# A network with a bidirectional Mamba as its last layer: a block's preparation in other steps of a hand-written schedule, outputs gated in place, GpSimd's products in other states

## The chip, the cores and the metric

One core of a Trainium2 chip runs the whole network in one launch. The time is device microseconds of the program; smaller is better. Engines are named as in the profile: PE (TensorE, matmul), DVE (VectorE), ACT (ScalarE), POOL (GpSimd), SP (SyncE, which here only issues DMAs). Each engine works through its own queue in order and waits on semaphores for the others.

## The reference

The input is (2, 128, 56, 56) in float32. Four layers, each added to its input: an agent attention, a 3x3 convolution, a mixture of experts on 2x2 patches, and a Mamba that runs in both directions along each row of the image. The change is in the last layer alone. Cut to what it computes, for one direction (`f` along the row, `b` against it), with L = 56, 256 inner channels and 16 states:

```python
xz = x @ in_w.T                       # x: (112 rows, 56, 128)
xi, z = jnp.split(xz, 2, axis=-1)
xc = silu(conv_b + sum(xp[:, k:k + L, :] * conv_w[:, k] for k in range(4)))
dt, Bm, Cm = jnp.split(xc @ xproj_w.T, [8, 24], axis=-1)
dt = softplus(dt @ dt_w.T + dt_b)
def step(h, inp):
    dt_l, B_l, C_l, u_l = inp
    h = exp(dt_l[:, :, None] * A) * h + (dt_l * u_l)[:, :, None] * B_l[:, None, :]
    return h, jnp.einsum('bds,bs->bd', h, C_l)
y = (ys + xc * Dp) * silu(z)
out = y @ out_w.T
```

Both directions' outputs are joined, multiplied by `fuse_w`, normalized over the channels and added to x.

## The kernel before, in words

**Blocks, ways, pairs, units.** The 112 rows of the two images are cut into 14 blocks of 8 rows (BLK = 448 positions). A block has two *ways*, f and b (class `Half`). A way has 16 *units*: unit u is the pair of states j = u // 2 and the half of the channels m = u % 2. The 128 partitions hold 64 channels times the two states of the pair, and the two groups of 64 channels (r) lie one after another, so that each unit works on 128x896 values. There are 14 x 2 x 16 = 448 units.

**What a unit does.** `decay` (L1820, ACT, twice 128x448): dA = exp(A dt), into one of two PSUM buffers. `push` (L1831, POOL): dBu = dtu times B, into one of four buffers. `scan` (L1853, DVE): the recurrence, into the tile h of the pair. After the second unit of a pair comes the *C product*, h times the row of C (128x1792): on DVE (L1862) it reads C from PSUM bank `c`, where `read_out` (L1841, PE) spreads it; on POOL (L1859), for the pairs listed in `POOLED`, it reads C from SBUF, where `send_low` has spread it by DMA (L1750). `collect` (L1873, PE) adds the two states and accumulates over the pairs into y in PSUM; the first one adds the skip term (L1869). After a way's last unit `close` (L1879, DVE) multiplies y by the Silu of the gate.

**What a way needs first.** `norm` (L1610, ACT; once for a block); `conv(0)`, `conv(1)` (L1703 PE, L1712 ACT); `silu` (L1884 to L1887, ACT: a table load, the Silu of this way's xc and, at the same time, of the block before's gates zs, and a table load back); `low` (PE, ACT L1735); `send_low` (SP: low to DRAM, then B and C spread to all partitions); `step(m)` (L1755 PE, four activations L1765 to L1769 on ACT); `error(m)` (L1775, DVE); `log(m)` (L1780, ACT); `softplus(m)` (L1785 PE, L1786 ACT); `weigh` (L1793, POOL: dtu = dt xc, into the tile `sp_u`; then a small memset of dt, L1797); `send_steps` (L1808, SP: four DMAs for dtu, four for dt, which bring them into the units' layout); `gate(m)` (L1720 PE, L1727 ACT).

**What follows a block.** `fuse` (L1624 PE, L1635 ACT), `measure` (L1641, L1643, DVE statistics), `root` (L1648, L1649, ACT), `newton` (L1657 to L1661, DVE), `normalize` (L1665, ACT), `turn_back` (L1676 PE, L1680 ACT), `onto` (L1686, POOL: the sum with x; L1688, the DMA out).

**What sets the order.** Within the scheduled part each engine's queue is the order in which the program text calls it. The main loop goes over the 448 units. For unit n it issues: `decay` of unit n+1; the *fetches* due at n (the copy out of PSUM that a stage before has left over); `push` of unit n+3; `scan` of unit n with its C product; `close` of a way that is through; `read_out` at even units of pairs not on POOL; `collect` of the unit three before (a quota lets it fall one behind at unit 3 and catch up later); then `run(n)`, the stages booked for step n. `book(at + k, ...)` puts a stage at step k counted from the start of the block before (32 steps a block: 0 to 15 its f units, 16 to 31 its b units, 32 and on the block's own units). `tag` says which of two PSUM banks the stage uses, `mm` or `c`, which it shares with the read-outs; its fetch comes one step later, or two with `late=1`. The tables of these steps, written by hand for the first block and in the `else` branch for all others, are what the change rewrites.

Buffers that matter: `sp_u` one for both ways, `zs` (the gates) one for f and two for b, `yv` (the gated output) one for each way, `Cs` one for each way with all its pairs, `Bs` two, `h` four, `dBu` four, `dA` two.

Of the kernel before, what the change touches and what calls it, by code (L numbers as in the profile page):

```python
# [8 lines left out]
F32 = mybir.dt.float32  # L9
# [1427 lines left out]

MAMBA_STATES, MAMBA_RANK, MAMBA_TAPS = 16, 8, 4

POOLED = {"f": (0, 3, 6), "b": (0, 3)}  # L1440


class MambaWeights:
# [88 lines left out]
def mamba_pair(net, out, wts, combine):  # L1532
# [19 lines left out]
    with ExitStack() as ctx:  # L1552
# [137 lines left out]
        class Half:  # L1690


            def __init__(self, blk, w):
                self.blk, self.w = blk, w
                self.dA, self.dBu, self.hc = {}, {}, {}

            def conv(self, m):
                w = self.w
# [17 lines left out]
            def gate(self, m):  # L1716
                pm = mm("gate_ps")
                if m == 0:
                    self.zs = work.tile([P, 2, BLK], F32, name="zs", tag=f"zs{self.w.d}", bufs=1 if self.w.d == "f" else 2)
                nc.tensor.matmul(  # L1720
                    rows(pm[:, :BLK]),
                    self.w.gate[:, m, :],
                    self.blk.xn[:, :, K - 1 : K - 1 + HW],
                    start=True,
                    stop=True,
                )
                return lambda: nc.scalar.copy(self.zs[:, m, :], pm[:, :BLK])  # L1727
# [8 lines left out]

            def send_low(self):

                pooled = self.w.pooled
                far = dram.tile([2 * S, BLK], F32, name="far", tag="far")  # L1740
                nc.sync.dma_start(far, self.lo[R:, :])
                self.B = work.tile([P, PAIRS, BLK], F32, name="Bs", tag="Bs")
                self.C = work.tile([P, len(pooled), BLK], F32, name="Cs", tag=f"Cs{self.w.d}", bufs=1)
# [90 lines left out]

            def read_out(self, u):

                r = R + S + u // 2 * 2
                self.c_ps = ps.tile([P, 512], F32, name="c_ps", tag="c")
                for s in range(2):
                    one_row = net.ident[:LOW, r + s : r + s + 1].to_broadcast([LOW, H])  # L1840
                    nc.tensor.matmul(self.c_ps[s * H : (s + 1) * H, :BLK], one_row, self.lo, start=True, stop=True)  # L1841

            def scan(self, u):

                j, m = self.unit(u)
                if m == 0:
                    self.hc[j] = work.tile([P, 2, 2, BLK], F32, name="h", tag="h", bufs=4)
                h = self.hc[j]
                hf, bf = (v.rearrange("p r t -> p (r t)") for v in (h[:, m], self.dBu[u]))
                af = self.dA[u][:, : 2 * BLK]  # L1850
                if self.w.d == "b":
                    hf, af, bf = hf[:, ::-1], af[:, ::-1], bf[:, ::-1]
                nc.vector.tensor_tensor_scan(hf, af, bf, 0.0, ALU.mult, ALU.add)  # L1853
                if m == 1:
                    shape = [P, 4, BLK]
                    h4 = h.rearrange("p m r t -> p (m r) t")
                    if self.by_pool(u):
                        c = self.C[:, self.w.pooled.index(j), :].unsqueeze(1).to_broadcast(shape)
                        nc.gpsimd.tensor_tensor(h4, h4, c, ALU.mult)  # L1859
                    else:  # L1860
                        c = self.c_ps[:, :BLK].unsqueeze(1).to_broadcast(shape)
                        nc.vector.tensor_tensor(h4, h4, c, ALU.mult)  # L1862

            def collect(self, u):
                j, m = self.unit(u)
# [9 lines left out]
                    )  # L1875

            def close(self):
                self.yv = work.tile([P, 2, BLK], F32, name="yv", tag=f"yv{self.w.d}", bufs=1)
                nc.vector.tensor_mul(self.yv, self.y[:, :, :BLK], self.zs)  # L1879

        def silu(inputs, gates):

            if inputs:
                nc.scalar.activation(inputs.xc, inputs.xc, AF.Silu)  # L1884
            if gates:
                nc.scalar.activation(gates.zs, gates.zs, AF.Silu)
            nc.scalar.preload_act_table_set(EXP_LN)  # L1887
# [5 lines left out]
        def book(step, *stages, tag="mm", late=0):  # L1893

            agenda.setdefault(step, []).extend((stage, tag, late) for stage in stages)

        for n, blk in enumerate(blocks):
# [31 lines left out]
                book(11, b.weigh, b.send_steps)  # L1929
            else:  # L1930
                before = blocks[n - 1]
                book(at + 6, blk.norm)
                book(at + 7, lambda f=f: f.conv(0))
                book(at + 8, lambda f=f: f.conv(1), late=1)
                book(at + 10, lambda f=f, g=before.ways[0]: silu(f, g))
                book(at + 12, lambda b=b: b.conv(0))
                book(at + 12, lambda b=b: b.conv(1), tag="c", late=1)
                book(at + 15, f.low, tag="c")
                book(at + 17, f.send_low)
                book(at + 17, lambda f=f: f.step(0))  # L1940
                book(at + 18, lambda b=b, g=before.ways[1]: silu(b, g))
                book(at + 19, lambda f=f: f.error(0))
                book(at + 19, lambda f=f: f.log(0))
                book(at + 20, lambda f=f: f.step(1))
                book(at + 21, lambda f=f: f.error(1))
                book(at + 22, lambda f=f: f.log(1))
                book(at + 22, lambda f=f: f.softplus(0), tag="c")
                book(at + 23, b.low)
                book(at + 24, lambda f=f: f.softplus(1))
                book(at + 25, f.weigh)  # L1950
                book(at + 26, lambda f=f: f.gate(0))
                book(at + 27, lambda b=b: b.step(0))
                book(at + 27, f.send_steps)
                book(at + 28, lambda b=b: b.error(0))
                book(at + 28, lambda b=b: b.log(0))
                book(at + 29, lambda b=b: b.step(1))
                book(at + 31, lambda b=b: b.error(1))
                book(at + 31, lambda b=b: b.log(1))
                book(at + 32, lambda b=b: b.softplus(0), tag="c")
                book(at + 33, lambda f=f: f.gate(1), late=1)  # L1960
                book(at + 33, lambda b=b: b.softplus(1), tag="c")
                book(at + 33, b.send_low)
                book(at + 35, lambda b=b: b.gate(0))
                book(at + 38, b.weigh)
                book(at + 43, b.send_steps)
                book(at + 46, lambda b=b: b.gate(1), late=1)

            at = STEPS * (n + 1)
            book(at + 4, lambda blk=blk: blk.fuse(0))
            book(at + 4, lambda blk=blk: blk.fuse(1), late=1)  # L1970
            book(at + 6, blk.measure)
            book(at + 7, blk.root, tag="c", late=1)
            book(at + 7, blk.newton)
            book(at + 15, blk.normalize)
            book(at + 16, blk.turn_back)
            book(at + 31, blk.onto)
        for h, step in zip(blocks[-1].ways, (10, 18)):
# [17 lines left out]
        with tc.manual_schedule(engines={E.PE, E.Activation, E.DVE, E.Pool, E.SP}):  # L1995
# [13 lines left out]
            for _ in second:  # L2009
                pass  # L2010
        with tc.manual_schedule(engines={E.PE, E.Activation, E.DVE, E.Pool, E.SP}):
            units[0][0].decay(0)
# [130 lines left out]
```

## Time and profile before

| | |
|---|---|
| median of 4 runs | 3104.88 us (3100.77 to 3114.65) |
| the profiled execution: time, span | 3106.7 us, 3104.9 us |
| granted TensorE clock over the span | 0.936 |
| the Mamba: first push; first scan; end of the last scan; last operation's end | 1736.8; 1738.9; 3077.0; 3092.8 us |
| start of scan 0 of the second block; of the last block | 1846.0; 2988.9 us |

The Mamba's 14 blocks take about 95 us each, the first 107. The page's busy times over the whole span mix the four layers; of the Mamba alone the groups of instructions, over the stretch from 2080 to 3000 us, say:

| line, engine, what | count | mean ns of one |
|---|---|---|
| L1831 POOL push, 128x896 | 310 | 2143 |
| L1853 DVE scan, 128x896 | 310 | 2006 |
| L1862 DVE C product, 128x1792 | 107 | 2021 |
| L1859 POOL C product, 128x1792 | 49 | 3992 |
| L1793 POOL weigh, 128x896 | 19 | 2108 |
| L1820 ACT dA, 128x448, two to a unit | 618 | 636 |
| L1884, L1887 ACT table loads | 38 | 1283 |
| L1879 DVE gating, 128x896 | 20 | 1084 |

Of the DMAs, dtu (224 KB) has a median of 3.9 us from issue to landing, dt 5.2, one C row pair's half (112 KB) 7.4, B (896 KB) 9.0. A mean is the time from an instruction's start to its end. Instructions that follow each other on an engine overlap a little, so their distance from start to start is a few hundredths of a microsecond less. A wait is put down to what released it last.

### The profile page before, as it was taken

To read this page: it belongs to the slowest core of one execution; us is meant where nothing else is said; L and a number is where in the kernel's file an instruction comes from. 1 tells how busy PE (TensorE), PEld (TensorE's weight loads), DVE (VectorE), ACT (ScalarE), POOL (GpSimd) and SP (SyncE) were. 2 spreads that over 40 slices of the span, in tenths; PEclk is the share of its full clock that TensorE was granted. 3 is DMA by queue.
4 is the path that set the end of the run, shared out by engine and by line. 5 is a ranking of instruction groups with operands and counts; after the bars stand their busy time and mean duration, and the time that the engine had idled before them with its cause. 6 is when DMAs were issued, how large, how long until landed. Compare 5 with 4: busy or idle time off the path is not lost. (4 is left out here: it accounts for less than half of the span.)

```text
span 3104.9 us, 34608 instructions
## 1 busy us (share of the span) xinstructions
PE 2822.4 (91%) x12964; PEld 1076.7 (35%) x12964; DVE 2225.3 (72%) x2033; ACT 1758.0 (57%) x2634; POOL 1500.3 (48%) x801
## 2 busy tenths in 40 slices
PE   7999999999898899999996789999889898889885
PEld 3333333332244444444443322333323333233321
DVE  5879999999886111111112699999999999999996
ACT  5778878877641011011111577776777777777764
POOL 3000100000511000000002799999999999999995
PEclk9999999999998899999997888989999999889987
DMA  1000000000011778777783553444444535434440
GB/s 54 1 1 1 1 1 1 1 1 1 1 36 44 309 284 318 293 308 308 290 316 104 114 103 81 91 103 93 96 89 87 105 82 114 91 81 91 95 101 8
DMA packets 133271, 333.65 MB, mean 107 GB/s; under 512 B 20228, under 2 KB 90340, under 8 KB 129492
## 3 DMA queue, kind: packets, MB, share of 16 engines
q1 hardware_dynamic: 111104, 303.96, 34.0%
q0 software_dynamic: 5520, 15.62, 1.6%
q10 hardware_dynamic: 16452, 11.61, 1.2%
q8 instruction: 106, 1.74, 0.2%
q14 instruction: 89, 0.73, 0.1%
HBM read 262.56 MB, written 17.20 MB: 90 GB/s over the span
## 5 line engine op out<-in xcount | busy, mean ns | idle before, releaser
L1831 POOL TENSOR_TENSOR dBu<-dtu,Bs 128x896 f32<-128x896 f32 x448 | 945.3, 2144 | 50.6 <-DVE h L1853 38.2
L1853 DVE TENSOR_TENSOR_SCAN h<-dA,dBu 128x896 f32<-128x896 f32 x448 | 879.0, 2007 | 59.4 <-ACT dA L1820 45.4
L620 ACT ACTIVATE ex<-sc 128x896 f32<-128x896 f32 (+1 forms) x700 | 602.6, 917 | 125.6 <-PE sc L617 114.2
L627 DVE TENSOR_TENSOR ex_sum<-ex_sum,ex 128x1792 f32<-128x1792 f32 (+1 forms) x238 | 492.6, 2070 | 35.3 <-ACT ex L620 21.2
L1873 PE MATMUL y<-h,both 128*64 128x448 f32 x1792 | 468.5, 624 | 16.1 <-POOL h L1859 15.0
L617 PE MATMUL sc<-q,k 32*128 32x448 f32 (+1 forms) x2800 | 404.2, 589 | 3.6 <-ACT ex L620 2.9
L1341 PE MATMUL h_ps<-w,xs_c 128*128 128x512 f32 x896 | 392.8, 596 | 10.3 <-issue 10.3
L1820 ACT ACTIVATE dA<-dt,f_A 128x448 f32<-128x448 f32 x448 | 284.5, 637 | 107.0 <-DVE h L1853 76.4
L635 PE MATMUL av<-ex,va 128*32 128x448 f32 (+1 forms) x2800 | 334.5, 552 | 0.1
L1862 DVE TENSOR_TENSOR h<-h,c_ps 128x1792 f32<-128x1792 f32 x154 | 311.3, 2021 | 26.3 <-PE c_ps L1841 11.6
L582 POOL TENSOR_TENSOR a_e<-a_e,a_inv 112x784 f32<-112x784 f32 x14 | 41.6, 2973 | 585.0 <-ACT ex L620 394.6
L1820 ACT ACTIVATE dA<-dt,b_A 128x448 f32<-128x448 f32 x448 | 283.8, 636 | 67.0 <-DVE h L1853 53.6
L1345 DVE TENSOR_TENSOR he<-h_ps,sg 128x512 f32<-128x512 f32 x56 | 38.6, 692 | 381.2 <-PE h_ps L1341 343.8
L1289 POOL DMA_INDIRECT xr<-xd,whom x28 | 28.1, 1003 | 535.3 <-PE xr_ps L1331 490.7
L1859 POOL TENSOR_TENSOR h<-h,Cs 128x1792 f32<-128x1792 f32 x70 | 279.7, 3995 | 2.3 <-DVE h L1853 2.3
L1841 PE MATMUL c_ps<-low,ident 40*64 40x448 f32 x616 | 173.2, 643 | 89.6 <-DVE h L1862 67.5
L1341 PEld LDWEIGHTS h_ps<-w,xs_c 128*128 128x128 f32 x896 | 168.7, 191 | 218.2 <-issue 202.5
L1873 PEld LDWEIGHTS y<-h,both 128*64 128x64 f32 x1792 | 116.5, 150 | 319.7 <-issue 250.4
L617 PEld LDWEIGHTS sc<-q,k 32*128 32x128 f32 (+1 forms) x2800 | 137.7, 181 | 230.3 <-issue 131.7
L1362 PE MATMUL o_ps<-w,ht 128*128 128x512 f32 x448 | 197.2, 592 | 0.4 <-ACT ht L1357 0.4
L1344 ACT ACTIVATE sg<-h_ps 128x512 f32<-128x512 f32 x56 | 33.4, 597 | 256.2 <-PE h_ps L1341 256.2
L1364 ACT ACTIVATE ot<-o_ps,share 128x512 f32<-128x512 f32 x28 | 19.2, 687 | 278.9 <-PE o_ps L1362 278.9
(334 smaller groups left out, 3059.4 us busy)
## 6 DMA issues: line engine op xcount, KB each, us to landing
w<-in_L_conv_w_dram SPq DMA_DIRECT2D x28, 4096.0 KB, 19.4
w<-in_L_conv_w_dram SPq DMA_DIRECT2D x28, 2048.0 KB, 10.3
Bs<-far SPq DMA_DIRECT2D x56, 896.0 KB, 9.0
dtu<-sp_u SPq DMA_DIRECT2D x108, 224.0 KB, 3.9
dt<-dt SPq DMA_DIRECT2D x108, 224.0 KB, 5.2
Cs<-far SPq DMA_DIRECT2D x140, 112.0 KB, 7.4
os<-ot ACTq DMA_DIRECT2D x28, 256.0 KB, 7.8
xd<-xt SPq DMA_DIRECT2D x14, 224.0 KB, 2.7
```

The source lines that it names most:

```text
L617: nc.tensor.matmul(sc[:size, j, :BLK], self.m.k[rows, at : at + size], self.q[rows, :], start=True, stop=True)
L620: nc.scalar.activation(ex[:size, 2 * g : 2 * g + 2, :], sc[:size, :, :BLK], AF.Exp, scale=scale)
L627: nc.vector.tensor_add(self.total[g][:size], self.total[g][:size], ex[:size])
L635: nc.tensor.matmul(self.av[rows, :BLK], self.m.va[:size, i, rows], self.ex[i][:size, h, :], start=i == 0, stop=i == STEPS - 1,)
L1341: nc.tensor.matmul(h_ps, xc[:, q, :], w1[:, q, f0 : f0 + 512], start=q == 0, stop=q == 3)
L1362: nc.tensor.matmul(o_ps, ht[:, i, :], w2[:, i, :], start=i == 0, stop=i == nj - 1)
L1820: nc.scalar.activation(self.dA[u][:, r * BLK : (r + 1) * BLK], self.dt2[:, m, r, :], AF.Exp, scale=self.w.A[:, j, 2 * m + r : 2 * m + r + 1],)
L1831: nc.gpsimd.tensor_tensor(self.dBu[u], self.dtu2[:, m], self.B[:, j, :].unsqueeze(1).to_broadcast(shape), ALU.mult)
L1853: nc.vector.tensor_tensor_scan(hf, af, bf, 0.0, ALU.mult, ALU.add)
L1859: nc.gpsimd.tensor_tensor(h4, h4, c, ALU.mult)
L1862: nc.vector.tensor_tensor(h4, h4, c, ALU.mult)
L1873: nc.tensor.matmul(self.y[r * H : (r + 1) * H, m, :BLK], both, self.hc[j][:, m, r, :], start=False, stop=j == PAIRS - 1)
```

## The change

In the text of `mamba_pair` and in one table ahead of it:

- The steps of almost all stages of blocks 1 to 13, and their banks and late marks, are others. So are those of what follows a block, and those of the last block's Silus (12 and 19 in place of 10 and 18). The first block's own table stays.
- POOL's C products: `POOLED` names units and no longer pairs. f: pairs 0 and 5, and the first half of pair 1. b: pairs 0 and 4, and the first half of pair 2. Before they were pairs 0, 3, 6 and pairs 0, 3. A split pair is done in two halves of 128x896, each after its own scan, one on POOL and one on DVE.
- C for POOL has its own stage, `send_c`, one pair at a time, six units ahead, from five buffers in place of one tile for each way.
- `close` writes its product into `zs` itself; `zs` of f has two buffers; `sp_u` has two.
- `collect` catches up at unit 7 in place of 5.

```diff
-POOLED = {"f": (0, 3, 6), "b": (0, 3)}
+POOLED = {"f": (0, 1, 2, 10, 11), "b": (0, 1, 4, 8, 9)}
...
-                    self.zs = work.tile([P, 2, BLK], F32, name="zs", tag=f"zs{self.w.d}", bufs=1 if self.w.d == "f" else 2)
+                    self.zs = work.tile([P, 2, BLK], F32, name="zs", tag=f"zs{self.w.d}", bufs=2 if self.w.d == "f" else 2)
...
-                    for n, j in enumerate(pooled):
-                        r = S + 2 * j + s
-                        nc.sync.dma_start(self.C[half, n, :], far[r : r + 1, :].to_broadcast([H, BLK]))
+            def send_c(self, j):
+                if not (self.by_pool(2 * j) or self.by_pool(2 * j + 1)):
+                    return
+                self.C[j] = work.tile([P, BLK], F32, name="Cs", tag="Cs", bufs=5)
+                for s in range(2):
+                    r = S + 2 * j + s
+                    nc.sync.dma_start(
+                        self.C[j][s * H : (s + 1) * H, :], self.far[r : r + 1, :].to_broadcast([H, BLK])
+                    )
...
-                    self.u = work.tile([P, 2, BLK], F32, name="sp_u", tag="sp_u", bufs=1)
+                    self.u = work.tile([P, 2, BLK], F32, name="sp_u", tag="sp_u", bufs=2)
...
-                return u // 2 in self.w.pooled
+                return u in self.w.pooled
...
-                if m == 1:
-                    shape = [P, 4, BLK]
-                    h4 = h.rearrange("p m r t -> p (m r) t")
-                    if self.by_pool(u):
-                        c = self.C[:, self.w.pooled.index(j), :].unsqueeze(1).to_broadcast(shape)
-                        nc.gpsimd.tensor_tensor(h4, h4, c, ALU.mult)
-                    else:
-                        c = self.c_ps[:, :BLK].unsqueeze(1).to_broadcast(shape)
-                        nc.vector.tensor_tensor(h4, h4, c, ALU.mult)
+                ours = [self.by_pool(v) for v in (2 * j, 2 * j + 1)]
+                if ours[0] == ours[1]:
+                    if m == 0:
+                        return
+                    shape, h4 = [P, 4, BLK], h.rearrange("p m r t -> p (m r) t")
+                else:
+                    shape, h4 = [P, 2, BLK], h[:, m]
+                if ours[m]:
+                    nc.gpsimd.tensor_tensor(h4, h4, self.C[j].unsqueeze(1).to_broadcast(shape), ALU.mult)
+                else:
+                    nc.vector.tensor_tensor(h4, h4, self.c_ps[:, :BLK].unsqueeze(1).to_broadcast(shape), ALU.mult)
...
-                self.yv = work.tile([P, 2, BLK], F32, name="yv", tag=f"yv{self.w.d}", bufs=1)
+                self.yv = self.zs
...
+                if u % 2 == 0 and n + 6 < len(units):
+                    who, i = units[n + 6]
+                    who.send_c(i // 2)
...
-                if u % 2 == 0 and not h.by_pool(u):
+                if u % 2 == 0 and not (h.by_pool(u) and h.by_pool(u + 1)):
                     h.read_out(u)
...
-                quota = 0 if u == 3 and n > 3 else 2 if u == 5 and n > 5 else 1
+                quota = 0 if u == 3 and n > 3 else 2 if u == 7 and n > 7 else 1
```

The steps of the `else` branch, before and after (c: bank `c`; l: late):

| stage | before | after | | stage | before | after |
|---|---|---|---|---|---|---|
| norm | 6 | 1 | | b.conv(0) | 12 | 12 |
| f.conv(0) | 7 | 7 | | b.conv(1) | 12 c l | 16 c l |
| f.conv(1) | 8 l | 9 c l | | silu(b, gates before) | 18 | 19 |
| silu(f, gates before) | 10 | 12 | | b.low | 23 | 25 c |
| f.low | 15 c | 13 c | | b.gate(0) | 35 | 20 |
| f.send_low | 17 | 16 | | b.step(0) | 27 | 26 l |
| f.step(0) | 17 | 15 | | b.error(0), b.log(0) | 28, 28 | 29, 29 |
| f.error(0), f.log(0) | 19, 19 | 17, 17 | | b.step(1) | 29 | 30 |
| f.step(1) | 20 | 22 | | b.softplus(0) | 32 c | 31 c l |
| f.softplus(0) | 22 c | 19 | | b.error(1), b.log(1) | 31, 31 | 32, 33 |
| f.error(1), f.log(1) | 21, 22 | 24, 24 | | b.softplus(1) | 33 c | 34 |
| f.softplus(1) | 24 | 25 | | b.send_low | 33 | 36 |
| f.weigh | 25 | 26 | | b.weigh | 38 | 38 |
| f.gate(0) | 26 | 27 c | | b.send_steps | 43 | 40 |
| f.send_steps | 27 | 27 | | b.gate(1) | 46 l | 41 |
| f.gate(1) | 33 l | 29 | | | | |

What follows a block, counted from the start of the next one: fuse 4 and 4 late, now 5 and 5 (c); measure 6, now 11; root 7 (c, late), now 13; newton 7, now 14; normalize 15, still 15; turn_back 16, now 21; onto 31, now 35.

More of the change, by code (lines that the diff above doesn't have):

```diff
@@ L1694, in __init__ @@
                 self.blk, self.w = blk, w
-                self.dA, self.dBu, self.hc = {}, {}, {}
+                self.dA, self.dBu, self.hc, self.C = {}, {}, {}, {}
             def conv(self, m):
@@ L1737, in send_low @@
             def send_low(self):
-                pooled = self.w.pooled
-                far = dram.tile([2 * S, BLK], F32, name="far", tag="far")
+                far = self.far = dram.tile([2 * S, BLK], F32, name="far", tag="far")
                 nc.sync.dma_start(far, self.lo[R:, :])
                 self.B = work.tile([P, PAIRS, BLK], F32, name="Bs", tag="Bs")
-                self.C = work.tile([P, len(pooled), BLK], F32, name="Cs", tag=f"Cs{self.w.d}", bufs=1)
                 for s in range(2):
@@ L1835, in read_out @@
             def read_out(self, u):
+                self.c_ps = ps.tile([P, 512], F32, name="c_ps", tag="c")
                 r = R + S + u // 2 * 2
-                self.c_ps = ps.tile([P, 512], F32, name="c_ps", tag="c")
                 for s in range(2):
@@ L1931, in mamba_pair @@
                 before = blocks[n - 1]
-                book(at + 6, blk.norm)
+                book(at + 1, blk.norm)
                 book(at + 7, lambda f=f: f.conv(0))
-                book(at + 8, lambda f=f: f.conv(1), late=1)
-                book(at + 10, lambda f=f, g=before.ways[0]: silu(f, g))
+                book(at + 9, lambda f=f: f.conv(1), tag="c", late=1)
+                book(at + 12, lambda f=f, g=before.ways[0]: silu(f, g))
                 book(at + 12, lambda b=b: b.conv(0))
-                book(at + 12, lambda b=b: b.conv(1), tag="c", late=1)
@@ L1938, in mamba_pair @@
[L1938 to L1952, printed above, removed]
-                book(at + 27, f.send_steps)
[L1954 to L1963, printed above, removed]
+                book(at + 13, f.low, tag="c")
+                book(at + 15, lambda f=f: f.step(0))
+                book(at + 16, lambda b=b: b.conv(1), tag="c", late=1)
@@ new lines, in mamba_pair @@
+                book(at + 16, f.send_low)
+                book(at + 17, lambda f=f: f.log(0))
+                book(at + 17, lambda f=f: f.error(0))
+                book(at + 19, lambda f=f: f.softplus(0))
+                book(at + 19, lambda b=b, g=before.ways[1]: silu(b, g))
+                book(at + 20, lambda b=b: b.gate(0))
+                book(at + 22, lambda f=f: f.step(1))
+                book(at + 24, lambda f=f: f.error(1))
+                book(at + 24, lambda f=f: f.log(1))
+                book(at + 25, b.low, tag="c")
@@ new lines, in mamba_pair @@
+                book(at + 25, lambda f=f: f.softplus(1))
+                book(at + 26, lambda b=b: b.step(0), late=1)
+                book(at + 26, f.weigh)
+                book(at + 27, lambda f=f: f.gate(0), tag="c")
+                book(at + 27, f.send_steps)
+                book(at + 29, lambda b=b: b.log(0))
+                book(at + 29, lambda b=b: b.error(0))
+                book(at + 29, lambda f=f: f.gate(1))
+                book(at + 30, lambda b=b: b.step(1))
+                book(at + 31, lambda b=b: b.softplus(0), tag="c", late=1)
@@ L1964, in mamba_pair @@
+                book(at + 32, lambda b=b: b.error(1))
+                book(at + 33, lambda b=b: b.log(1))
+                book(at + 34, lambda b=b: b.softplus(1))
+                book(at + 36, b.send_low)
                 book(at + 38, b.weigh)
-                book(at + 43, b.send_steps)
-                book(at + 46, lambda b=b: b.gate(1), late=1)
+                book(at + 40, b.send_steps)
+                book(at + 41, lambda b=b: b.gate(1))
             at = STEPS * (n + 1)
-            book(at + 4, lambda blk=blk: blk.fuse(0))
@@ L1970, in mamba_pair @@
[L1970 to L1973, printed above, removed]
+            book(at + 5, lambda blk=blk: blk.fuse(0))
+            book(at + 5, lambda blk=blk: blk.fuse(1), tag="c")
+            book(at + 11, blk.measure)
+            book(at + 13, blk.root)
+            book(at + 14, blk.newton)
             book(at + 15, blk.normalize)
-            book(at + 16, blk.turn_back)
@@ L1976, in mamba_pair @@
-            book(at + 31, blk.onto)
-        for h, step in zip(blocks[-1].ways, (10, 18)):
+            book(at + 21, blk.turn_back)
+            book(at + 35, blk.onto)
+        for h, step in zip(blocks[-1].ways, (12, 19)):
             book(STEPS * (len(blocks) - 1) + step, lambda h=h: silu(None, h))
@@ L2011, in mamba_pair @@
         with tc.manual_schedule(engines={E.PE, E.Activation, E.DVE, E.Pool, E.SP}):
+            for h, u in units[:6:2]:
+                h.send_c(u // 2)
             units[0][0].decay(0)
```

## The prediction

> **What bounds the kernel now.** The span of the profiled execution is 3104.9 us (its own time 3106.7, the median of the runs 3104.88, so terms worked out in the span are added to the median as they are). The change touches the last stage alone, from the first push at 1736.8 us to the end. I read GpSimd (POOL) first, because over the twelve steady blocks (1838 to 2981 us, 95.25 us each) it is busy 1106.1 of 1143 us, VectorE (DVE) 1078.8, and TensorE 1034.0. The waits of POOL and of DVE in that stretch:
>
> ```profile
> POOL dBu L1831 <- DVE h L1853: 30.6, 34, 2.1
> POOL dBu L1831 <- DMA dtu<-sp_u: 3.4, 10, 0.7
> POOL dBu L1831 <- DMA dt<-dt: 0.9, 1, 0.9
> ...
> DVE h L1853 <- ACT dA L1820: 37.6, 34, 2.0
> DVE h L1862 <- PE c_ps L1841: 5.8, 12, 0.9
> ```
>
> The columns are the total, the number and the longest in us. Two engines run nearly full and hand each other work: POOL makes a unit's input (a push), DVE scans it, and the push of unit n+4 waits until scan n has freed one of four buffers. POOL loses 2.9 us a block, nearly all because a scan came late, and scans come late because ScalarE (ACT) was late with dA. Then POOL's queue in time, around the place where the forward way of the next block begins:
>
> ```profile
> 2300.47 4.21 POOL L1831 TENSOR_TENSOR dBu<-dtu,Bs 128x896 f32<-128x896 f32 x2
> 2304.65 2.07 POOL L1793 TENSOR_TENSOR sp_u<-dt,xc 128x896 f32<-128x896 f32 x1
> 2306.78 0.13 POOL L1797 MEMSET dt<- 128x16 f32 x1
> 2306.84 6.29 POOL L1831 TENSOR_TENSOR dBu<-dtu,Bs 128x896 f32<-128x896 f32 x3
> 2314.08 4.21 POOL L1831 TENSOR_TENSOR dBu<-dtu,Bs 128x896 f32<-128x896 f32 x2 [0.95 <-DMA dt<-dt]
> ```
>
> This is the row that decides. `weigh` (L1793) makes dtu, `send_steps` copies it across partitions by DMA, and the first push of the next way needs the copy. Three pushes fit between, and even so POOL waits 0.95 us here. Over the twelve blocks this wait is (3.4+0.9)/12 = 0.36 us.
>
> **The change, part by part.** *POOL's work.* Start to start, when nothing waits, a push takes 2.094 us (10.47 for five), a whole C product 3.945, weigh with its memset 2.25, onto 1.09. Before: 32 x 2.094 + 5 x 3.945 + 2 x 2.25 + 1.09 = 92.3 us a block, and with the 2.9 of waits 95.2, the period. After: four whole products and two halves, f two and a half pairs, b too. A half has the shape of a push, 128x896 with one operand broadcast; between half of 3.945 (1.97) and a long push (2.18) I take the push, 2.09. So 92.3 - 3.945 + 2 x 2.09 = 92.55 us, +0.24 a block (0 to +0.4). VectorE gets the same sum, ten pairs and two halves for eleven pairs, some 0.1 us more for gaps.
>
> *The moved weigh.* `f.weigh` goes from step 25 to 26, and pushes stand in the queue one per step: now unit 13's push is ahead of it and only two, 14 and 15, lie between it and the next way's first. The copies start when weigh ends, wherever `send_steps` (still 27) stands. In front of them on SP now stand two C transfers of the next block's pair 0, which need `far` from step 16 and a buffer whose product ended five products ago, so nothing waits there. From the end of the memset to the push is 3 x 2.094 + 0.36 = 6.64 us. Two pushes fill 4.19, so POOL must wait 2.45 us every block (2.2 by the shortest of the waits, 3.0 by the 0.95). Behind that push stands everything POOL does. Nothing hides it: the cycle from the first push to weigh's end and through the copy is 92.55 - 4.19 + 6.64 = 95.0 us, whatever the other engines do.
>
> The Trainium skill speaks differently of the copy: its page "DMA: Bandwidth & Descriptors", section "Anatomy of one DMA — SWDGE (gpsimd) path", gives about 2.0 us fixed and bytes over 436e3 for one DMA, 2.5 us for 224 KB. By an estimate from that, with the three issues before the last at 0.69 us, POOL would wait about 0.4 us in place of 2.45, and the total would be some 25 us lower. The page fits another issuing path, and the row of this case has 3.9 us from issue to landing, so the row is used.
>
> *The waits that go.* At step 18 ACT runs four activations of `step` (2.35 us), then both table loads and Silus (4.4 us), and DVE stood 1.97 us for dA; at the other Silu, step 10, 0.83 us. After, the Silus are at 12 and 19: at 12 the statistics (1.05) and at 19 the gating (1.0) and a product (2.04) lie on DVE between the scans, and no `step` is fetched there. From the end of scan 18: dA 1.3, Silus 4.4, dA 1.3 makes 7.0 for the dA of unit 21, and DVE needs 1.95 + 1.95 + 2.04 + 1.0 to begin scan 20 and 6.9 for scan 21. So these 2.8 us a block go. A second `sp_u` buffer takes away ACT's wait for the copy of dtu (3.8 us at 2218.85), which cost DVE 0.5. DVE's work of some 90 us then has 5 us of room in 95.0, and the 30.6 us that POOL waited for scans (2.55 a block) can go. They are what pays for the 2.45.
>
> *A new lateness.* The next way's first dA needs dt, whose four copies follow dtu's on SP: the last issue is at 2217.5 and lands 5.3 later, 10.4 us after the memset's end at 2212.44. With one dA (1.3) scan 0 starts 10.4 + 1.3 - 6.65 = 5.1 us after its push, and ends 7.1 after it; push 4 is due at 4 x 2.094 = 8.4. Queued behind that dA on ACT are the four activations of `b.step(1)` (fetched at 31), dA 1 and 2, `log` and `norm`: by their rows they hold scans 1 and 3 back by 1.55 us in all. To the end of scan 16 DVE has 17 scans at 1.95, five products at 2.04, a half (1.05), gating, error, statistics and Newton (1.0, 0.55, 1.05, 0.6): 47.6 us, so 5.1 + 47.6 + 1.55 = 54.3. POOL's push 20 is due at 20 x 2.094 + 2 x 3.945 + 2.09 + 1.09 + 2.25 = 55.2. The room is 1.3 us at push 4, 0.9 at push 20 and, counted on in the same way, 1.5 at push 28. Waits for scans: between 0 and the 2.55 a block of now; I take 0.25.
>
> *Free in the sum.* Gating in place: the buffer is read by `fuse` at step 5 and written by `gate` from 20 on, two buffers apart. One more read-out pair a block (twelve pairs need c_ps, not eleven) is 0.97 us of TensorE, covered by its 9 us of idle time a block; if that cover were gone, 14 x 0.97 = 14 us. `far`, B and C leave in other places on SP, each C 6 units (some 17 us) ahead of a transfer that lands in 7.4.
>
> *Ends of the stage.* In block 0 `b.weigh` (step 11, not moved) now stands behind the product of f's pair 5. That product needs scan 11; following the queue from the 1766.0 at which scan 7 ended, weigh ends near 1786.6 (1781.6 before) and b's first push starts near 1793.2 (1789.1), with half a product less behind it: +3.5 us (0 to +5). In the last block no weigh of a next block stands on POOL and no error on DVE; scan 31 was 3.6 us behind its push there, and DVE begins nearer to POOL: -2.3 us (-3.5 to 0). The rest of the tail has the same instructions.
>
> **Sum.** Twelve blocks at 95.0 + 0.25 against 95.25 give 0; with the ends, +3.5 and -2.3, it is +1.2, so 3106 us. No difference that can be measured: at 0.3% (9.3 us, about what a measurement of this kernel can tell from no change) the bounds are 3095.6 and 3114.2.
>
> **The rivals.** *The copy is quicker or hidden (faster).* If the wait before a way's first push stays 0.36 us, the gain is 30.6 less 12 x 0.24 and the ends: 3105 - 30.6 + 2.9 + 1.2 = 3078; with half of it, 3092. For it: DVE's waits have named causes that the change removes. Against it: no transfer competes there now either, and all 11 waits show the copy as the last to come.
>
> *The scans stay late (slower).* Place: the first scans of the forward way and the stretch around push 20. If ACT, blocked by dt's landing, holds DVE more than the 0.9 us of room at push 20, each further us is a us a block, on top of the copy. If POOL still waits 2.55 us for scans, the block is 95.0 + 2.55 = 97.55: 12 x 2.3 + 1.2 = +29, 3134 us; with half of them, 3120. For it: the room is small in three places and my sums leave semaphores out. Against it: DVE loses its two largest waits.
>
> *TensorE becomes late (slower).* It is 90% busy and its order changes most; a product that waits for c_ps delays every later scan. In the present profile a gap of 2.8 us before 2282.36 was followed by 4.3 us at a granted clock of 0.72 and 0.55, where four skip instructions took 3.09 us. Some 1 us a block gives +14: 3120. Against it: products wait only 5.8 us in twelve blocks, and the two conv stages of b, now in one step, are taken apart.
> The skill's "TensorE: Matmul & The Clock Gate", Part 1, lets the clock drop only after an idle window of about 3.4 us. By it a gap of 2.8 us costs nothing; the row shows a drop, so it is not used.
>
> **How the numbers follow.** No change by POOL's cycle: 0.45, own range 3096 to 3114. Copy quicker: 0.20. Scans or TensorE late: 0.35 (0.22 and 0.13). Faster by over 0.3% therefore 0.20, within 0.45, slower 0.35. The range takes half of the gain and most of the losses: 3090 to 3130; outside it lie about 0.08 below and 0.12 above.
>
> **What would show it.** Right: POOL's wait for dtu before a forward way's first push grows from 0.36 to about 2.4 us in each block, its waits for scans fall under 5 us in all, DVE's for dA to under 20, and a steady block stays within 0.5 us of 95.25. Wrong: a dtu wait under 1.2 us (then 3092 or less), or waits for scans above 15 us (then 3115 or more), or c_ps waits above 15 us.

## The result, and the profile after

The changed kernel takes 3102.82 us (median of 43 runs, 3099.82 to 3109.38) against 3108.12 of the kernel before (69 runs on the same chips, 3100.77 to 3118.12). The ratio is 0.9984, 95% interval 0.9980 to 0.9988: some 5 us quicker (3.7 to 6.2). That is less than the 0.3% which the prediction took for the least that can be told from no change, but over so many runs it is a gain, and 1.2 us of loss had been forecast.

GpSimd's waits in the twelve steady blocks, 1838 to 2981 us, of the changed kernel (total, number, longest):

```profile
POOL dBu L1835 <- DMA dtu<-sp_u: 32.7, 13, 4.0
POOL h L1866 <- issue: 1.8, 5, 1.0
POOL dBu L1835 <- DVE h L1857: 0.7, 1, 0.7
```

This is the mirror of before: the copy of dtu now holds nearly all of it (3.4 before), and the pushes' waits for scans, 30.6 before, are gone but for 0.7. The 13 waits stand at the first pushes of blocks 1 to 13; the twelve of blocks 1 to 12 are 30.4 us, 2.53 a block. GpSimd's queue where the forward way of a block begins (start, length):

```profile
2303.51 2.07 POOL L1797 TENSOR_TENSOR sp_u<-dt,xc 128x896 f32<-128x896 f32 x1
2305.64 0.13 POOL L1801 MEMSET dt<- 128x16 f32 x1
2305.70 4.23 POOL L1835 TENSOR_TENSOR dBu<-dtu,Bs 128x896 f32<-128x896 f32 x2
2312.82 8.40 POOL L1835 TENSOR_TENSOR dBu<-dtu,Bs 128x896 f32<-128x896 f32 x4 [2.89 <-DMA dtu<-sp_u]
```

Two pushes fill the copy, not three. VectorE in the same stretch:

```profile
DVE h L1857 <- ACT dA L1824: 35.8, 49, 2.8
DVE h L1868 <- PE c_ps L1845: 4.1, 6, 1.1
```

The total for dA is hardly lower than before (37.6), but it sits elsewhere. VectorE's idle time ahead of its scans, by unit: before, 1.99 us a block at unit 20 and 0.81 at unit 12, behind the Silus; after, 1.76 at unit 0 and 0.67 at unit 1 of the way that begins, and 0.5 behind the Silus.

The span taken apart, from the starts of pushes in each trace. A profile is one execution, so the kernels were profiled more than once; the right two columns are the changed kernel with only the first way's C transfers reordered, whose steady blocks are the same code:

| us | before | before (e16) | before (e17) | after | after (e13) | e1 | e14 |
|---|---|---|---|---|---|---|---|
| first push | 1736.8 | 1732.6 | 1736.1 | 1730.8 | 1731.6 | 1734.5 | 1733.4 |
| block 0 | 100.8 | 107.8 | 108.0 | 105.4 | 110.8 | 104.4 | 103.9 |
| second block's first push | 1837.6 | 1840.5 | 1844.1 | 1836.3 | 1842.4 | 1838.9 | 1837.3 |
| a steady block, mean of 12 | 95.25 | 95.55 | 95.55 | 95.12 | 94.95 | 95.03 | 94.89 |
| last block, to the end of the last scan | 96.4 | 96.4 | 96.0 | 95.4 | 95.0 | 94.7 | 94.8 |

A steady block is 95.45 before and 95.0 after in the mean of these columns, 12 x 0.45 = 5.4 us; the last block gives another 1.3. That is a little more than the 5 us of the timed runs. Block 0 spreads by several us in both kernels, so what it adds or takes is not shown. The executions of e16 and e17 took longer than the median of the kernel before, but their steady block is not an exception: it is 95.55 in e8 below too, an execution of 3107.9 us whose blocks differ from the kernel before only in where C's transfers stand on SyncE.

### The profile page after: what moved, and what is told of

Same layout as the page of the kernel before. It is cut to its first block, busy times and chain, and to the rows that moved or that the text cites. A ratio compares the mean times of both kernels' runs of the same rounds, so it can differ in the third digit from the quotient of the medians.

```text
span 3100.9 us, 34827 instructions
## 1 busy us (share of the span) xinstructions
PE 2816.1 (91%) x13020; PEld 1076.1 (35%) x13020; DVE 2231.0 (72%) x2047; ACT 1751.4 (56%) x2634; POOL 1500.9 (48%) x815
## 5 line engine op out<-in xcount | busy, mean ns | idle before, releaser
L1835 POOL TENSOR_TENSOR dBu<-dtu,Bs 128x896 f32<-128x896 f32 x448 | 943.9, 2138 | 45.6 <-DMA dtu<-sp_u 41.5
L1879 PE MATMUL y<-h,both 128*64 128x448 f32 x1792 | 434.6, 593 | 20.5 <-POOL h L1866 13.8
L1868 DVE TENSOR_TENSOR h<-h,c_ps 128x1792 f32<-128x1792 f32 (+1 forms) x168 | 313.5, 1866 | 22.6 <-PE c_ps L1845 5.5
L1345 DVE TENSOR_TENSOR he<-h_ps,sg 128x512 f32<-128x512 f32 x56 | 38.5, 691 | 380.1 <-PE h_ps L1341 343.2
L1866 POOL TENSOR_TENSOR h<-h,Cs 128x1792 f32<-128x1792 f32 (+1 forms) x84 | 282.0, 3357 | 4.3 <-issue 2.7
L1879 PEld LDWEIGHTS y<-h,both 128*64 128x64 f32 x1792 | 106.0, 142 | 318.7 <-issue 249.3
```

Of the source, the lines that this page charges most:

```text
L1835: nc.gpsimd.tensor_tensor(self.dBu[u], self.dtu2[:, m], self.B[:, j, :].unsqueeze(1).to_broadcast(shape), ALU.mult)
L1866: nc.gpsimd.tensor_tensor(h4, h4, self.C[j].unsqueeze(1).to_broadcast(shape), ALU.mult)
L1868: nc.vector.tensor_tensor(h4, h4, self.c_ps[:, :BLK].unsqueeze(1).to_broadcast(shape), ALU.mult)
L1879: nc.tensor.matmul(self.y[r * H : (r + 1) * H, m, :BLK], both, self.hc[j][:, m, r, :], start=False, stop=j == PAIRS - 1)
```

## The experiments

The ratios are to the kernel before, run beside each experiment. Steps are those of the table of the change.

**Where did the gain come from: the start?** By the two recorded profiles the start of the stage was the missed term: from the last memset's end to the first push, which needs dtu, it is 4.06 us in place of 9.59 (2.4 us of each are GpSimd's own issuing of dt's copies). The C transfers no longer stand ahead of the first dtu copies.

e1, the changed kernel with the first pairs' four transfers issued ahead of dtu:

```diff
                 book(at + 9, f.send_low)
+                for j in range(3):
+                    book(at + 9, lambda f=f, j=j: f.send_c(j))
...
-            for h, u in units[:6:2]:
-                h.send_c(u // 2)
```

> The changed kernel, but the first way's four C transfers stand on SP ahead of the first copies of dtu again, as C stood before. Theory: the kernel gained its 5 us at the start of the stage, where the first push came 6.0 us earlier because dtu landed in 3.6 to 5.0 us (7.0 to 10.3 before). Then the first push starts 3 to 5 us later than in the changed kernel (1734 to 1736 us) and the total rises by about as much, less what block 0 hides behind other waits: 3104 to 3108 us. Rival: the gain is the steady blocks', whose scans are no longer late; then the total stays within 1.5 us of 3102.8.

Measured 3102.89, ratio 0.9979 (0.9968 to 0.9990). The first push came 8.23 us behind the memset, and nothing was lost at the end.

e8, the reverse: the kernel before with the first way's C transfers behind its dtu copies (a `send_c` of all pairs, called after them), and in every other way behind both transfers of B.

> The kernel before with C's transfers behind B's in every way, and in the first way of all behind the copies of dtu. If the start of the stage is what the change gained by: the first push comes 4 to 6 us earlier (its wait falls from 9.6 to 4 to 5 us) and the total falls by 3 to 6 us. If block 0 swallows it, as the run with C ahead suggests: the first push comes earlier and the total stays within 2 us of the kernel before.

Measured 3106.82, ratio 0.9988 (0.9979 to 0.9998), the first push 5.13 us behind the memset. That is about 3.7 us of gain (0.6 to 6.5), so the two runs disagreed. e13 is the changed kernel again, e14 the changed kernel with all six transfers (pairs 0, 1, 5) ahead, on the same chip.

> The changed kernel once more, for a comparison on one chip with the next run. Ratio to before 0.998 to 0.999 (some 3102 to 3106 us), first push at 1730 to 1731 us, second block's first push near 1836.3.

> The changed kernel with all six C transfers of the first way issued ahead of its dtu copies, as in the kernel before. Both theories: the first push waits 9 to 10 us for dtu in place of 4.06. Theory S (the start's gain reaches the end; it is the term left out of the prediction): the second block's first push comes 3 to 5 us later than in the run of the changed kernel beside it, and the median is 3 to 5 us higher, near the kernel before. Theory B (block 0 swallows it, because its own waits set when the second block begins): the second block's first push within 1 us, and the median within 2 us of the run beside it.

Measured 3103.43 (0.9979, 0.9969 to 0.9989) and 3101.44 (0.9982, 0.9973 to 0.9991). In e14 the first push comes 9.45 us behind the memset, and the total is no higher: in the changed kernel block 0 swallows the start. Half of it is gone by the second push, which needs the second half of dtu: in the changed kernel it waits another 2.69 us and starts 8.9 us behind the memset, in e14 it does not wait and starts at 11.5. e13's second block began 6.1 us later than in the recorded profile of the same kernel, which was not expected; TensorE's clock goes with it (last section). What e8 gained in the kernel before stays open: its steady block is 95.55, so the 3.7 us are not there, and its one profile cannot part the start from the spread of block 0.

e16 and e17, the kernel before profiled twice more, to see its steady block in other executions:

> The kernel before once more, for its profile. The changed kernel's steady block was 95.12, 94.95 and, in the two runs that only reorder its start, 95.03 and 94.89 us, mean 95.0. Theory T (the 5 us rest on the steady blocks and the tail): the steady block is 95.3 to 95.6 here, GpSimd's waits for scans 25 us or more in twelve blocks, and from the last block's first push to the end of the last scan 96 to 97 us, so that 12 x 0.4 + 1.4 gives the gain. Theory B0 (they rest on block 0): the steady block is 95.0 to 95.2, and the second block's first push comes at 1840 us or later.

> The same once more: theory T a steady block of 95.3 to 95.6 us, theory B0 one of 95.0 to 95.2 and a second block that begins at 1840 us or later.

Measured one execution each, 3113.14 and 3116.48 us. Steady block 95.55 in both, as theory T says, with these waits of GpSimd in e16's blocks:

```profile
POOL dBu L1831 <- DVE h L1853: 33.7, 35, 2.1
POOL dBu L1831 <- DMA dtu<-sp_u: 3.1, 9, 0.6
```

The second blocks begin at 1840.5 and 1844.1, as theory B0 says of this kernel, but the changed kernel's begin anywhere from 1836.3 to 1842.4, so these profiles show no sure gain at that point. The steady blocks and the last block carry a difference of the size of the gain, and the profile the forecast was made from was the quickest of the three executions.

**Is the moved weigh the price?** e3 moves it one step further, with one push left to fill the copy; e4 makes the step 25 to 26 alone, in the kernel before.

```diff
-                book(at + 26, f.weigh)
+                book(at + 27, f.weigh)
```

> The changed kernel with f.weigh one step later (27): one push is left to cover the copy. Theory: one push more of waiting in every block, 95.1 + 2.1 = 97.2 us, and 3128 us in all; POOL's waits for scans stay near 0. Rival (the wait for dtu falls together with a wait for scans, so that its length costs little): under 3115 us.

> The kernel before with this one step of the change alone: f.weigh at 26 in place of 25. Theory: POOL's cycle through the copy becomes 92.3 - 4.2 + 6.6 = 94.7 us, but VectorE, which was 5.2 us late a block for dA, is not helped, so that part of the waits for scans (2.55 us) stay: between 95.3 (all of them hidden behind the copy) and 97.3 us a block, 3106 to 3130, most likely about 3113. Rival: the two waits exclude each other and the time stays within 3 us of the kernel before.

e3: 3128.98, ratio 1.0065 (1.0045 to 1.0085), dtu wait 4.5 a block, block 97.15. One push less to fill the copy costs 2 us a block. e4: 3133.37, ratio 1.0076 (1.0056 to 1.0096), block 97.5. GpSimd's waits in e4:

```profile
POOL dBu L1831 <- DVE h L1853: 30.7, 33, 2.1
POOL dBu L1831 <- DMA dtu<-sp_u: 26.7, 11, 2.7
```

Both waits stand side by side: 30.7 for scans is what it was (30.6), and the copy's came on top. But in e4 the copy holds VectorE as well:

```profile
ACT sp_u L1780 <- DMA dtu<-sp_u: 72.3, 12, 6.6
DVE h L1853 <- ACT dA L1820: 61.0, 33, 3.3
```

The kernel before has one `sp_u`, and ScalarE's `log` for the b way must wait until the copy has read it: 72.3 us, 43.2 before. VectorE's waits for dA grow by 23.4 us, all of it at unit 30 (2.70 us a block, 0.54 before), just ahead of the push for which GpSimd waits. So VectorE cannot catch up in that time, and e4 prices the moved weigh together with the single buffer; whether both waits would stay with two buffers in the old schedule was not run. By e3, with two buffers, a push less is 2.0 us a block. In the change the wait for the copy grew by 2.2 us a block, and the rest of the edits pay for it.

**Then put weigh back?** e2, the changed kernel with weigh at 25 and the stages ahead of it one step earlier:

```diff
-                book(at + 24, lambda f=f: f.error(1))
-                book(at + 24, lambda f=f: f.log(1))
+                book(at + 23, lambda f=f: f.error(1))
+                book(at + 23, lambda f=f: f.log(1))
...
-                book(at + 25, lambda f=f: f.softplus(1))
+                book(at + 24, lambda f=f: f.softplus(1))
...
-                book(at + 26, f.weigh)
+                book(at + 25, f.weigh)
...
-                book(at + 27, f.send_steps)
+                book(at + 26, f.send_steps)
```

> The changed kernel with f.weigh one step earlier (25), and what feeds it too (f.error(1), f.log(1) at 23, f.softplus(1) at 24), so that three pushes cover the copy of dtu. Theory (POOL's cycle binds, the new wait of 2.5 us is the price of the step): the wait before a forward way's first push falls to about 0.4 us, the steady block from 95.1 to 93.0 us, the total by 12 x 2.1 = 25 us to 3078. Rival (VectorE, with 90.5 us of work and 3.3 us of waits a block, is bound right behind): the block falls to 93.8 only and POOL waits for scans again, 3087 us. If neither engine's cycle is what binds, 3100 or more.

Measured 3109.8, ratio 0.9996 (0.9984 to 1.0009), block 95.6: neither theory nor rival. GpSimd's waits:

```profile
POOL dBu L1835 <- DVE h L1857: 18.1, 25, 1.4
POOL h L1866 <- issue: 13.7, 10, 1.7
POOL dBu L1835 <- DMA dtu<-sp_u: 3.7, 10, 1.6
```

The copy's wait is gone (0.3 a block) and waits for scans are back. The C products' wait, whose releaser the profile does not name ("issue"), is one for a scan too: it is at the forward way's first product, which in each block starts 0.13 us after scan 1 has ended. VectorE waits for ScalarE's dA at units 1 and 3 of the way that begins (0.67 and 1.55 us a block), and GpSimd meets the lateness there and again at pushes 20 and 28. The copy was not the only limit, it was the later of two.

**Relieve ScalarE at the way's start.** e5, the changed kernel with b.step(1) a step earlier and norm three later; e6 the same with weigh at 25.

```diff
-                book(at + 1, blk.norm)
+                book(at + 4, blk.norm)
...
-                book(at + 30, lambda b=b: b.step(1))
+                book(at + 29, lambda b=b: b.step(1))
```

> The changed kernel with ScalarE relieved at the start of the forward way: b.step(1) at 29 in place of 30, so that its four activations (2.35 us) stand ahead of the first dA, which waits for the copy of dt, and norm at 4 in place of 1. Theory (two cycles of nearly the same length are tied together: POOL's through the copy of dtu, 95.0 us, and VectorE's with its waits for dA, some 95.5): POOL's cycle still binds, the wait for dtu stays 2.4 us, and the total stays within 3 us of 3102.8. Rival (VectorE's waits at the way's start are the cost, the copy is not): 1 to 2 us a block go, 3080 to 3091.

> Both: f.weigh at 25 and the relief. With weigh alone POOL's wait for dtu fell to 0.3 us, but VectorE waited 0.36 + 0.67 + 1.55 us for ScalarE before units 0, 1 and 3, POOL then waited for it, and a block took 95.6 us. Theory of two tied cycles: only both edits together shorten it, by most of these 2.6 us, to 93.0 to 93.9 us a block, 3079 to 3090 us. Rival (the waits for ScalarE only move to later units): 3100 or more.

e5: 3091.19, ratio 0.9940 (0.9926 to 0.9955), block 94.37, better than both kernels. The theory had said 3100 or more; GpSimd's wait for dtu did stay at 2.5 us a block, as it said, and VectorE's waits for dA fell from 35.8 to 18.6 us. Of the 0.6 us a block that e5 gains on the 95.0, most is that the pushes of this execution lie closer together (last section), which no run ties to the edit. e6: 3095.85, ratio 0.9951 (0.9936 to 0.9965), block 95.0, a miss: VectorE now waited 2.02 us a block for c_ps at the product of unit 31. TensorE's queue there in e6, where the first push of the way starts at 2310.1:

```profile
2310.47 1.86 PE L1720 MATMUL gate_ps<-pad,f_gate_t 128*128 128x448 f32 x2 [3.27 <-DVE sp_e L1779]
2312.95 1.86 PE L1759 MATMUL dt_ps<-low,b_dt_t 8*128 8x448 f32 x2 [0.62 <-ACT zs L1727]
2314.74 1.76 PE L1845 MATMUL c_ps<-low,ident 40*64 40x448 f32 x4
```

f.gate(1), booked at 29 too, waits 3.27 us for b.error(0) to free bank `mm`; b.step(1) waits for ScalarE's copy of the gate out of that bank; the read-out stands behind both. So f.gate(1) had to leave. e9 and e10 are the two edits of e5 each alone; e11 is e5 with the gate at 36, e12 is e11 with weigh at 25:

```diff
-                book(at + 29, lambda f=f: f.gate(1))
...
                 book(at + 36, b.send_low)
+                book(at + 36, lambda f=f: f.gate(1))
```

> The changed kernel with one of the two edits of the relief alone: the next block's norm at step 4 in place of 1. The relief run was 11 us quicker than the changed kernel. Theory A (the four activations of b.step(1) are what keeps VectorE late at a forward way's start, norm is a fifth of the ScalarE work there): a steady block of 95.0 us or more, total within 3 us of the changed kernel, 3100 to 3106. Theory B (norm's activation and what it takes from PE and ScalarE just behind dA 1 is the cause): a block near 94.4 us, 3089 to 3094. Under both GpSimd's wait for dtu before a forward way's first push stays at 2.4 to 2.6 us a block.

> The changed kernel with the other edit alone: b.step(1) booked at step 29 in place of 30, so that its four activations stand on ScalarE ahead of the dA that waits for the copy of dt. Theory A: nearly all of the relief's gain, a block of 94.4 to 94.6 us, 3090 to 3095. Theory B: 3100 to 3106. If the two edits only work together (each alone under a third of the gain), both runs are above 3099.

> The relief with f.gate(1) at step 36 in place of 29, so that TensorE meets no wait for ScalarE's copy of the gate ahead of b.step(1) and of the read-out for unit 31. Theory A (GpSimd's own cycle with the wait for the copy of dtu sets the block; VectorE has some room): VectorE's wait for c_ps at the product of unit 31 (1.06 us a block in the relief) falls under 0.3, but the block stays at 94.2 to 94.5 us and the total at 3088 to 3094. Theory B (VectorE and GpSimd still hand lateness to each other): a block under 94.0, total under 3087.

> The same with f.weigh at step 25 and the stages ahead of it one step earlier, so that a third push fills the copy of dtu. GpSimd's work without that wait is 94.37 - 2.5 = 91.9 us a block by the relief run, VectorE's about 90.5. Theory A (once TensorE and ScalarE are not blocked at the way's start, the wait for the copy can be filled without VectorE becoming late): a block of 92.2 to 93.5 us, dtu wait under 0.6, waits for scans under 1 us a block, total 3066 to 3082. Theory B (the third push only exchanges the wait for the copy for waits for scans, as in the two runs with weigh at 25 before): a block of 94.3 to 95.2, total 3089 to 3099.

e9: 3101.47 (0.9976, 0.9966 to 0.9985), block 94.96, hardly a gain. e10: 3097.6 (0.9967, 0.9954 to 0.9979), block 94.58. b.step(1) is what relieves VectorE: its waits for dA are 18.7 us in e10 and 36.9 in e9. The times of the two are not told apart, e10's lies between what the two theories had said, and e5's median is 6 us lower than e10's. e11: 3100.25 (0.9979, 0.9967 to 0.9992), block 94.99, a miss: with weigh at 26 the copy's wait still sets the block, and clearing TensorE's queue gives nothing. It is even slower than e5. Unit 0's dA is later there (1.86 us a block against 0.92), but the 0.6 us are made of the pushes' distance and of GpSimd's waits for scans, some 0.3 each. e12: 3074.07, ratio 0.9891 (0.9875 to 0.9908), block 93.1, as its theory A said. In e12 the way's first push starts at 2298.08:

```profile
2298.43 1.86 PE L1759 MATMUL dt_ps<-low,b_dt_t 8*128 8x448 f32 x2 [3.16 <-DVE sp_e L1779]
2300.22 1.76 PE L1845 MATMUL c_ps<-low,ident 40*64 40x448 f32 x4
```

The read-out starts 2.1 us after the push, in e6 4.6. And GpSimd:

```profile
2289.24 2.16 POOL L1797 TENSOR_TENSOR sp_u<-dt,xc 128x896 f32<-128x896 f32 x1
2291.46 0.13 POOL L1801 MEMSET dt<- 128x16 f32 x1
2291.52 6.32 POOL L1835 TENSOR_TENSOR dBu<-dtu,Bs 128x896 f32<-128x896 f32 x3
2298.08 10.48 POOL L1835 TENSOR_TENSOR dBu<-dtu,Bs 128x896 f32<-128x896 f32 x5 [0.24 <-DMA dtu<-sp_u]
```

Three pushes in the gap, 0.24 us of wait, and hardly a wait for scans takes its place (1.3 us at pushes in twelve blocks): 6.9 us of VectorE's waits for dA are left, of 35.8. The pushes lie as far apart as in the changed kernel, so this gain is the schedule's. e15 moves b.weigh of block 0 from step 11 to 10 in e12, ahead of the product of pair 5:

> The kernel of e12 with b.weigh and its copies at step 10 in place of 11 in the first block, ahead of the product of f's pair 5. If GpSimd's 4.3 us wait there for the copy reaches the end: 2 to 5 us quicker than e12, 3069 to 3072 us. If VectorE sets the pace of block 0, as its scans run later than that: within 1.5 us of e12, 3072 to 3076.

Measured 3073.27, ratio 0.9880 (0.9865 to 0.9895), not told apart from e12's. GpSimd's 4.3 us there are gone, and in block 0 its pushes' waits for scans rose from 3.1 to 5.8 us in their place: b's dtu in block 0 is not what the end waits for.

**What is the second `sp_u` buffer worth?** e7 takes it away in the changed kernel (`bufs=1`).

> The changed kernel with one sp_u buffer again: b.log(0) at step 29 writes the tile that the copy of f's dtu still reads, which lands about when the next way's first push starts. The prediction set this edit at 0.5 us of VectorE a block and covered. If ScalarE is blocked until then (6.6 us behind weigh, that is 5 us after its turn), the dA of unit 31 comes 2 to 4 us late, of which the wait for dt hides most: 0.3 to 2 us a block, 3106 to 3127. Rival: hidden, within 3 us of 3102.8.

Measured 3152.57, ratio 1.0133 (1.0119 to 1.0148), block 98.98. Waits of ScalarE and VectorE in e7's blocks:

```profile
ACT sp_u L1784 <- DMA dtu<-sp_u: 68.7, 12, 6.2
DVE sp_e L1779 <- ACT sp_u L1784: 43.3, 12, 4.1
```

ScalarE's `log` stands 5.7 us a block for the copy, and VectorE's `error` stands 3.6 behind the log. In the schedule before, the first wait was there too (43.2 us in all), but b.error(0) was issued ahead of b.log(0) and did not meet it; the change has them the other way round. So one buffer would cost the new schedule nearly 50 us. No run turns the order of the two back.

## Why the prediction was off, by its own steps

- **The moved weigh.** "From the end of the memset to the push is 6.64 us ... POOL must wait 2.45 us every block": measured 2.53. Right, and e3 (one push fewer in the gap) and e12 (one more) show it from both sides.
- **Pushes, products and halves.** A half product of 128x896 took 2.04 us from start to start (2.09 from start to end), 0.05 less than priced. The steady block came to 95.0, the floor worked out before any wait for scans.
- **The waits that go.** Those of pushes for scans went, all but 0.7 us. The products' 1.8 us ("issue") are waits for scans too: each such product starts 0.13 us after a scan has ended. Together that is 0.2 us a block, and 0.25 had been left for it. Right.
- **The step that failed** is the line "Twelve blocks at 95.0 + 0.25 against 95.25 give 0". Measured, it is 95.0 against 95.45, or 5.4 us of gain. The 95.25 was one execution's; in two others of the same kernel it was 95.55, and the mean of the three makes 2.4 us of the 5.4. The 95.0 + 0.25 was 0.25 too dear, 3.0 us in all: the halves make up 0.1 of it, and for the rest no single row answers. The mechanism was right, and the difference of two nearly equal terms was taken to be known better than one execution can tell.
- **Ends of the stage.** The +3.5 for block 0 was +4.7 in the recorded pair, but the first push came 6.0 us earlier, which the prediction left out, so the second block began 1.3 us earlier and not 3.5 later. e14 shows that this start is not a gain in itself: with the transfers back ahead, the total is no higher. What is left of the +3.5 cannot be read, as block 0 spreads by more from one execution to the next; e15 shows that b's weigh behind the product, the reason given, costs nothing that can be told in e12's schedule. "-2.3" for the last block was -1.0, and -1.3 in the mean of the profiles.
- **DVE's waits for dA under 20 us**: wrong, 35.8. The new lateness was described at its place, unit 0, GpSimd's room at push 4 was right (under 0.1 us of wait there), and so was scan 0, 5.0 us behind its push (5.1 worked out). But the 2.4 us a block that VectorE stands there are waits for dA as well, 29 us in all, and the sign left them out. They were hidden because GpSimd waited 2.5 us for the copy at the same place: in e2, without that wait, scans are late again.
- **The rivals.** "The copy is quicker or hidden", 3078 us, is what the experiments reached in the end (3074), but not by the copy alone: e2 took that wait away and gained nothing against the kernel before. "The scans stay late" did not happen in the changed kernel; in e2 they are late, but in place of the copy's wait and not on top of it. "TensorE becomes late": products waited 4.1 us for c_ps, less than before, and the granted clock over these blocks rose from 0.91 to 0.94. The gate that held TensorE up in e6 is the same mechanism in a place that was not named.
- **The second sp_u** was put at 0.5 us a block; e7 puts its worth in the new schedule at 4 us a block. The prediction priced what the old schedule lost, not what the new one would lose without it.
- The Trainium skill's page "DMA: Bandwidth & Descriptors", section "Anatomy of one DMA — SWDGE (gpsimd) path", would have left a wait of 0.4 us by the estimate in the prediction; 2.53 was measured, so setting that page aside for another issuing path was right.

## What to carry to other kernels

When two limits lie close together, taking away the one that the waits show only uncovers the other: find, for the engine that was waiting, who else was late at that moment, and move both. Price a buffer or a wait in the schedule that will be there, not in the one that is profiled. And where a forecast is the difference of two periods, take the period before from several executions; here they differed by 0.3 us, 3.6 us over twelve blocks.

## What was not expected of the hardware

**TensorE's clock in block 0 differs between executions of one kernel.** Windows of the changed kernel, the recorded profile and then e13 (busy us and counts of PE, PEld, DVE, ACT, POOL; then granted clock, DMA share, GB/s):

```profile
1750.00:1762.00 12.00, 9.95 (x37) 2.83 (x34) 9.82 (x7) 7.91 (x15) 12.00 (x7) 1.00 0.61 122
```

```profile
1750.00:1762.00 12.00, 11.38 (x23) 2.48 (x22) 7.95 (x5) 4.66 (x9) 12.00 (x7) 0.58 0.67 133
```

At a clock of 0.58 TensorE did 23 matmuls where it did 37, and ScalarE and VectorE were held up behind it: from 1740 to 1775 ScalarE waited 5.4 us for the gates' matmuls in e13, 0.9 in the other, and VectorE's `error` 7.2 us for ScalarE, 2.5 in the other. In both the stage began with a gap of 2.99 us on TensorE (until 1739.3 and 1739.7), and 1740 to 1750 ran at 0.68 and 0.67; only then did they part. The kernel before shows the same: 0.84 in the execution with a block 0 of 100.8 us, 0.57 and 0.50 in those of 107.8 and 108.0. So some 5 to 7 us of block 0's spread between executions goes with that clock, as much as the change is worth or more. The Trainium skill, "TensorE: Matmul & The Clock Gate", Part 1, says that the activity window runs freely and that the point of change varies with it, which fits; it puts the release at about 3.4 us of sustained work, while in e13 TensorE was busy 9.0 of the 10 us to 1750 and all of the next 10, and those ran at 0.50.

**Pushes of one shape keep another distance in some executions.** From start to start, where nothing waits, the median is 2.094 to 2.096 us in the changed kernel, e12 and two of the three profiles of the kernel before. It is 2.082 in the third of these (e17), 2.087 and 2.088 in e11 and e10, and 2.073 to 2.076 in e8, e7 and e5. The same kernel on the same chip had 2.094 (e16) and 2.082 (e17), so neither the kernel nor the chip sets it alone; what does was not found. In e5 the 0.02 us are 0.6 us in the 32 pushes of a block, and with the wait for the copy in GpSimd's cycle they bring the block below the floor of 95.0. In the kernel before they bring nothing: e16, e17 and e8 all have a block of 95.55, and the waits for scans grow from 33.7 to 38.5 and 41.5 us as the pushes move closer. There the scans, not the pushes, set the pace.
